# Graph layers on one core: the first six loads in halves on two queues, and one bank's identity products moved

## Chip, cores and metric

The kernel runs on one core of a Trainium2 chip. The metric is device time of one execution in microseconds (us), lower is better. The core has a matrix engine (TensorE, PE, with its weight load PEld), a vector engine (VectorE, DVE), an activation engine (ScalarE, ACT), GpSimd (POOL) and a queue engine (SyncE, SP). Loads are issued on the queues of SP and ACT, and a few on POOL's.

## The reference, cut to what matters

`x` is 16 x 1024 x 128 and `adj` is 1024 x 1024, both fp32. Layer 0 is one graph convolution with a residual and a layer norm. Layer 1 is five steps of a gated recurrent update whose messages are `adj @ h`, again with a residual and a layer norm:

```python
def _L0_gnn_ref(x, adj, weight, bias):
    support = jnp.einsum('bnf,fo->bno', x, weight)
    return jnp.einsum('nm,bmo->bno', adj, support) + bias

def step(h, _):                       # five times; in_matrix = out_matrix = adj
    m_in = jnp.einsum('nm,bmd->bnd', in_matrix, h)
    m_out = jnp.einsum('nm,bmd->bnd', out_matrix, h)
    av = jnp.concatenate([m_in, m_out], axis=-1)
    u3 = h @ u3_w.T + u3_b
    z = sigmoid(av @ w3_w.T + w3_b + u3)
    r = sigmoid(av @ w4_w.T + w4_b + u3)
    hv = tanh(av @ w5_w.T + w5_b + (r * h @ u5_w.T + u5_b))
    return (1.0 - z) * h + z * hv, None

x = _layernorm(x + _L0_gnn_ref(x, adj, L0_gnn_weight, L0_gnn_bias))
x = _layernorm(x + _L1_gnn_ref(x, adj, adj, ...))
```

## The kernel before, in words

The batch is worked in four groups of four ("quads"). For each quad the product with `adj` is done by a fast scheme in two levels with seven products each: outer matrices 1 to 7, and inside each of them inner products 1 to 7. `chain` runs the inner products of one or two outer matrices; its matrix instructions are line L410. First comes layer 0 for the four quads (chains `12_x0`, `3_x0`, `67_x0`, `54_x0` and so on), then five steps of layer 1 for each quad.

Before the first product can run, `adj` has to be on the chip and turned. It comes in eight **chunks** of 128 rows (0.524 MB each), chunks 0 to 3 into `agg`, 4 to 7 into `hid`; the rows of the first quad of `x` come as four loads of the same size, x0 to x3, into `rows`. The loop at lines 127 to 133 issues these twelve loads in the order chunk 0, chunk 1, x0, x1, chunks 2 to 7, x2, x3; the first six alternate between the queues of SP and ACT, the rest go on SP. Eight semaphores serve the loads in rotation, so that the ninth load waits in its queue for the landing of the first, the tenth for the second, and so on.

`make_identity` builds `ident` on POOL. Then PE multiplies `ident` by `ident` into three PSUM banks, `pb`, `seeded0` and `seeded1` (L212, four instructions for each bank; the trace has two records for each). This writes each bank once; later products add to these banks. After that `turn_adj(c)` (L200) turns a chunk with eight transposes into two banks `pt_adj`, four in each, and copies each bank to `a`, for chunks 0 to 3 the first on DVE (L205) and the second on ACT (L207), for chunks 4 to 7 both on ACT. Three PSUM banks take turns for this, so every fourth bank waits for the copy of the first.

PE's order in the first chain is kept as written in the program: the identity products, chunks 0 and 1, inner product 1 (called **P1** here, on `pa_x`, from chunks 0 and 1 and x0), then `first_rest` with chunks 2 and 3, inner product 2 (**P2**, on `pa_x`), then `turn_rest` with chunks 4 to 7, then inner product 5 (on `pc_x`), 6, 7, 3 and 4. P1 and P2 need chunks 0 and 1 alone; P2 stands behind the transposes of chunks 2 and 3 by its place in the order. On DVE the sums of x0 and x1 (L328 to L331) come between the copies; with L188 begins a long row of sums of the turned `adj`, of which the first waits for chunk 3. On ACT the load of a function table and a small copy `warm` (L137) follow its three load issues. L708 on ACT scales `rows` of x2 and x3 for a sum that POOL's queue completes.

Of the kernel before, what the change touches and what calls it, by code (L numbers as in the profile page):

```python
# [20 lines left out]
def kernel(  # L21
# [32 lines left out]
    nc = tc.nc  # L54
    B, N, D = x.shape
    P = 128
# [15 lines left out]
    rows = const.tile([P, QUAD, N], F32, name="rows")  # L72
# [16 lines left out]
    seeded = [ps_m.tile([P, HALF], F32, name=f"seeded{i}") for i in range(2)]  # L89
    pb = ps_m.tile([P, HALF], F32, name="pb")  # L90
# [24 lines left out]
    def x_rows(b):  # L115
        return x[b].rearrange("(p c) d -> p (c d)", c=C)
# [5 lines left out]
    queues = (nc.sync, nc.scalar)  # L122

    adj_rows = adj.rearrange("(h p n c) m -> n h p c m", h=2, n=4, c=2)
    raws = [agg[:, c] if c < CH else hid[:, c - CH] for c in range(C)]

    for i, c in enumerate([0, 1, "x0", "x1", *range(2, C), "x2", "x3"]):
        queue = queues[i % 2 if i < 6 else 0]
        if isinstance(c, str):
            k = int(c[1])  # L130
            queue.dma_start(rows[:, k], x_rows(k))
        else:
            queue.dma_start(raws[c], adj_rows[c // 2, c % 2])
    power = const.tile([P, C], F32, name="power")
    nc.vector.memset(power, -0.5)
    warm = const.tile([P, 1], F32, name="warm")
# [2 lines left out]
    ident = const.tile([P, P], F32, name="ident")  # L139
# [44 lines left out]
    def inner_left_12():  # L184
        a = [[blk[0][:, :, 2 * j : 2 * j + 2, ts(i, QT)] for j in range(2)] for i in range(2)]
        put = tc.keep_in_program_order
        (a11, a12), (a21, a22) = a
        put(nc.vector.tensor_sub(e12[:, :, 3], a11, a21))  # L188
        put(nc.vector.tensor_add(e12[:, :, 0], a21, a22))
        put(nc.vector.tensor_sub(e12[:, :, 1], e12[:, :, 0], a11))  # L190
        put(nc.vector.tensor_sub(e12[:, :, 2], a12, e12[:, :, 1]))

    def turn_adj(c):
        cols = raws[c].rearrange("p (q k) -> p k q", k=C)
        i, at = divmod(c, CH)
        for j in range(2):
            pt = bank(f"pt_adj_{c}_{j}")
            pt3 = pt.rearrange("p (k q) -> p k q", k=CH)
            for k in range(CH):
                op = nc.tensor.transpose(pt3[:, k, :], cols[:, j * CH + k, :], ident)  # L200
                if c < CH:
                    tc.keep_in_program_order(op)
            dst = blk[i][:, j, :, ts(at, P)]
            if j == 0 and i == 0:
                tc.keep_in_program_order(nc.vector.tensor_copy(dst, pt3))  # L205
            else:
                nc.scalar.copy(dst, pt3)  # L207


    for t in (pb, *seeded):  # L210
        for k in range(CH):
            nc.tensor.matmul(t[:, ts(k, P)], ident, ident, start=(k == 0), stop=True,  # L212
                             skip_group_check=True)
    for c in range(2):
        turn_adj(c)

# [525 lines left out]
        )  # L742

    def first_rest():
        for c in range(2, CH):
            turn_adj(c)
        inner_left_12()
# [184 lines left out]
    for q in range(NQ):  # L932
        for s in range(STEPS):
# [21 lines left out]
            k = s if q else s - 1  # L955
# [92 lines left out]
```

## Time and profile before

| | |
|---|---|
| median of 3 runs | 1767.29 us (1767.14 to 1767.44) |
| the profiled execution | 1767.04 us |
| its span, first to last instruction | 1765.1 us |
| granted TensorE clock | 0.999 |
| PE busy | 1755.0 us (99%) |
| DVE busy | 1302.0 us (74%) |
| ACT busy | 800.7 us (45%) |
| POOL busy | 108.2 us (6%) |
| moved by DMA | 161.86 MB, mean 92 GB/s |

The span is measured inside the execution; the 1.9 us between it and the execution's own time lie around the program. Busy time of PE is from records whose ends are modelled, so the starts of its records, and the waits of the engines around it, say more than its share. The views used below are the totals of the engines, the chain of work that ended last (the whole of it and its first 30 us), the timeline, the table by stages, and the list of load issues with the time from issue to landing.

### The profile page before, as it was taken

What the parts mean: (1) busy time and instruction counts of PE and PEld (TensorE: products, weight loads), DVE (VectorE), ACT (ScalarE), POOL (GpSimd) and SP (SyncE); (2) the same over time, 40 slices, a digit from 0 to 9 for tenths busy, and PEclk for the clock granted to TensorE, in tenths of its full rate; (3) what the DMA queues carried; (4) which work ended last, traced back from release to release, by engine and by line L of the source; (5) the groups of instructions that cost most, each with busy time, mean ns of one, the idle gap of its engine ahead of it and who ended that gap; (6) DMA issues with size and microseconds to landing.
All of it is one profiled execution on the core that took longest, in us unless ns stands there. A gap on an engine that the chain in (4) does not pass through costs nothing.

```text
span 1765.1 us, 19956 instructions
## 1 busy us (share of the span) xinstructions
PE 1755.0 (99%) x6709; PEld 1265.5 (72%) x6709; DVE 1302.0 (74%) x2286; ACT 800.7 (45%) x1425; POOL 108.2 (6%) x153
## 2 busy tenths in 40 slices
PE   9999999999999999999999999999999999999998
PEld 8888885776858577685867758586675857668584
DVE  7977777676776857777778667777778577777778
ACT  4355564344353433435354452535445353443537
POOL 2212320000000000000000000000000000000004
PEclk9999999999999999999999999999999999999999
DMA  8244354051322505143351424324243241514232
GB/s 267 72 142 144 120 142 109 12 119 33 87 67 69 140 18 136 39 119 73 83 132 60 108 60 96 87 69 119 58 110 101 55 93 26 131 25 107 60 84 95
DMA packets 405604, 161.86 MB, mean 92 GB/s; under 512 B 388352, under 2 KB 389504, under 8 KB 405504
## 3 DMA queue, kind: packets, MB, share of 16 engines
q1 hardware_dynamic: 402960, 153.01, 34.2%
q0 software_dynamic: 1968, 5.77, 1.3%
q10 hardware_dynamic: 576, 1.84, 0.3%
q8 instruction: 53, 0.87, 0.2%
q14 instruction: 47, 0.39, 0.1%
HBM read 94.51 MB, written 65.01 MB: 90 GB/s over the span
## 4 chain that ended last, share of the span: by engine, by line
PE 99%; DVE 0%; POOL 0%; POOLq 0%; issue 0%; DVEq 0%
PE pb L410 25%; PE pc L410 14%; PE pa L410 14%; PE pu L538 8%; PE ph L561 8%; PE ph L562 8%; PE pu L520 8%; PE seeded L553 8%; PE pa_x L410 3%; PE pc_x L410 3%; PE seeded L494 2%; PE pt_adj L200 0%; PE seeded L212 0%; PE pt L652 0%; PE pb L212 0%; PE pt_end L923 0%
## 5 line engine op out<-in xcount | busy, mean ns | idle before, releaser
L410 PE MATMUL pb<-e,inner 128*128 128x256 f32 x864 | 206.2, 379 | 0.0
L577 DVE TENSOR_TENSOR tsum<-tsum,hid 128x512 f32<-128x512 f32 x158 | 108.7, 688 | 106.1 <-ACT tsum L572 106.0
L572 ACT ACTIVATE tsum<-ph,bh 128x512 f32<-128x512 f32 x158 | 108.5, 687 | 164.6 <-PE ph L562 164.5
L410 PEld LDWEIGHTS pb<-e,inner 128*128 128x128 f32 x864 | 167.6, 194 | 19.0 <-ACT first L396 0.3
L538 PE MATMUL pu<-agg,w_t 128*128 128x512 f32 x320 | 163.7, 593 | 0.0
L561 PE MATMUL ph<-agg,w_t 128*128 128x512 f32 x320 | 163.4, 592 | 0.0
L553 PE MATMUL seeded<-agg,w_t 128*128 128x512 f32 x320 | 163.4, 592 | 0.0
L562 PE MATMUL ph<-tsum,u_t 128*128 128x512 f32 x320 | 163.4, 592 | 0.0
L520 PE MATMUL pu<-hid,u_t 128*128 128x512 f32 x320 | 157.0, 592 | 0.0
L541 ACT ACTIVATE tsum<-pu,br 128x512 f32<-128x512 f32 x160 | 110.0, 687 | 85.6 <-PE pu L538 85.6
L410 PE MATMUL pb<-s,inner 128*128 128x256 f32 x576 | 148.4, 380 | 0.0
L410 PE MATMUL pb<-a,inner 128*128 128x256 f32 x576 | 144.0, 379 | 0.0
L548 DVE TENSOR_TENSOR tsum<-tsum,hid 128x512 f32<-128x512 f32 x160 | 110.2, 689 | 37.7 <-ACT tsum L541 37.7
L410 PE MATMUL pc<-e,inner 128*128 128x256 f32 x560 | 133.9, 379 | 0.0
L410 PEld LDWEIGHTS pb<-s,inner 128*128 128x128 f32 x576 | 110.3, 194 | 24.8 <-issue 10.4
L556 ACT ACTIVATE tsum<-seeded,bz 128x512 f32<-128x512 f32 x160 | 110.0, 687 | 29.5 <-PE seeded L553 29.5
L410 PEld LDWEIGHTS pb<-a,inner 128*128 128x128 f32 x576 | 111.8, 194 | 12.7 <-DVE first L398 0.4
L410 PEld LDWEIGHTS pc<-e,inner 128*128 128x128 f32 x560 | 109.2, 195 | 12.8 <-issue 0.7
L562 PEld LDWEIGHTS ph<-tsum,u_t 128*128 128x128 f32 x320 | 60.8, 190 | 76.5 <-issue 58.8
L561 PEld LDWEIGHTS ph<-agg,w_t 128*128 128x128 f32 x320 | 60.6, 190 | 75.1 <-issue 74.4
L520 PEld LDWEIGHTS pu<-hid,u_t 128*128 128x128 f32 x320 | 60.8, 190 | 73.5 <-issue 72.2
L578 DVE TENSOR_TENSOR tsum<-tsum 128x512 f32<-128x512 f32 x158 | 109.2, 691 | 4.9
(197 smaller groups left out, 2860.2 us busy)
## 6 DMA issues: line engine op xcount, KB each, us to landing
turned<-ypad SPq DMA_DIRECT2D x48, 512.0 KB, 3.8
rows<-turned SPq DMA_DIRECT2D x192, 128.0 KB, 2.9
hvs<-saved SPq DMA_DIRECT2D x24, 512.0 KB, 4.0
rows<-saved SPq DMA_DIRECT2D x20, 512.0 KB, 3.7
hid<-hidden SPq DMA_DIRECT2D x64, 128.0 KB, 3.5
turned<-ypad SPq DMA_DIRECT2D x32, 256.0 KB, 2.9
rows<-turned SPq DMA_DIRECT2D x128, 64.0 KB, 2.1
hidden<-ypad SPq DMA_DIRECT2D x12, 512.0 KB, 4.1
```

The lines of the kernel that those rows point to most:

```text
L410: product = nc.tensor.matmul(bank_of[a][:, ts(o, QT)], chunk(a, o, c), left[n][a][:, c, :], start=(a in (1, 5) and o == 0 and c == 0), sto ...
L520: in_order(nc.tensor.matmul(pu, w_t["u3"], hid[:, k, ts(h, HALF)], start=True, stop=True, skip_group_check=True))
L538: in_order(nc.tensor.matmul(pu, w_t["w4"], agg[:, k, cols], start=False, stop=True, skip_group_check=True))
L541: pin(nc.scalar.activation(rh[:, cols], pu, AF.Sigmoid, bias=br))
L548: pin(nc.vector.tensor_mul(rh[:, cols], rh[:, cols], hid[:, k, cols]))
L553: in_order(nc.tensor.matmul(pz, w_t["w3"], agg[:, k, cols], start=False, stop=True, skip_group_check=True))
L556: pin(nc.scalar.activation(z_of[k % 2][:, cols], pz, AF.Sigmoid, bias=bz))
L561: in_order(nc.tensor.matmul(ph, w_t["w5"], agg[:, k, cols], start=True, stop=False))
L562: in_order(nc.tensor.matmul(ph, w_t["u5"], rh_of[k % 2][:, cols], start=False, stop=True))
L572: pin(nc.scalar.activation(hv, ph, AF.Tanh, bias=bh))
L577: pinned(nc.vector.tensor_sub(hv, hv, hid[:, k, cols]))
L578: pinned(nc.vector.tensor_mul(hv, hv, z_of[k % 2][:, cols]))
```

## The change

Each of the first six loads becomes two: the first half of the partitions (0 to 63) is issued on SP's queue, the second half (64 to 127) on ACT's. The source is divided to match; for a chunk of `adj` it is 32 of the 64 row pairs. The other six loads stay whole, on SP's queue. The identity products of `seeded1` leave their place ahead of chunk 0 and come at the start of `first_rest`, between P1 and chunk 2. They keep their place in the program's order, as do now those of the other two banks.

```diff
     for i, c in enumerate([0, 1, "x0", "x1", *range(2, C), "x2", "x3"]):
-        queue = queues[i % 2 if i < 6 else 0]
         if isinstance(c, str):
             k = int(c[1])
-            queue.dma_start(rows[:, k], x_rows(k))
+            dst, src = rows[:, k], x_rows(k)
+            halves = [src[ts(h, P // 2)] for h in range(2)]
         else:
-            queue.dma_start(raws[c], adj_rows[c // 2, c % 2])
+            dst, src = raws[c], adj_rows[c // 2, c % 2]
+            halves = [src[ts(h, P // 4)] for h in range(2)]
+        if i < 6:
+            for h, queue in enumerate(queues):
+                queue.dma_start(dst[ts(h, P // 2)], halves[h])
+        else:
+            nc.sync.dma_start(dst, src)
...
-    for t in (pb, *seeded):
+    def write_bank(t):
         for k in range(CH):
-            nc.tensor.matmul(t[:, ts(k, P)], ident, ident, start=(k == 0), stop=True,
-                             skip_group_check=True)
+            tc.keep_in_program_order(nc.tensor.matmul(
+                t[:, ts(k, P)], ident, ident, start=(k == 0), stop=True, skip_group_check=True
+            ))
+
+    write_bank(pb)
+    write_bank(seeded[0])
     for c in range(2):
         turn_adj(c)
...
     def first_rest():
+        write_bank(seeded[1])
         for c in range(2, CH):
             turn_adj(c)
         inner_left_12()
```

On the built program nothing else moves: the instructions of PE, DVE, ACT and POOL stand in the same order as before except the four of `seeded1`, and SP and ACT have three load issues more each. The loads now come as eighteen; with eight semaphores in rotation the halves of chunk 2 wait for the halves of chunk 0, those of chunk 3 for those of chunk 1, chunks 4 and 5 for the two halves of x0, chunks 6 and 7 for those of x1, and x2 and x3 for those of chunk 2.

## The prediction

> **What bounds the kernel now.** I began with the engine totals and the chain that ended last, over the whole span. This shows that TensorE (PE) carries the time; any change at the start counts only as far as it moves PE.
>
> ```profile
> PE 1755.0 (99%) x6709; PEld 1265.5 (72%) x6709; DVE 1302.0 (74%) x2286; ACT 800.7 (45%) x1425; POOL 108.2 (6%) x153
> ...
> PE 99%; DVE 0%; POOL 0%; POOLq 0%; issue 0%; DVEq 0%
> ```
>
> Then the same chain over the first 30 us (start, length, what). It is PE work from 1.35 us on, with one visible break: the VectorE (DVE) copy of chunk 1 before P1 (the first product, on `pa_x`).
>
> ```profile
> 1.35 2.08 PE pb L212 x8
> 3.43 3.41 PE seeded L212 x16
> 6.84 1.62 PE pt_adj L200 x12
> 8.47 0.02 issue
> 8.49 0.70 DVE a L205
> 9.19 0.04 issue
> 9.24 1.99 PE pa_x L410 x8
> 11.23 2.14 PE pt_adj L200 x16
> 13.37 1.73 PE pa_x L410 x8
> 15.10 3.84 PE pt_adj L200 x32
> 18.94 1.73 PE pc_x L410 x8
> ```
>
> After 26 us the timeline of PE has no gap that a load explains: product follows product at 0.216 us a record. So a shift of PE at about 15 us reaches the end undiminished. Everything that follows is: by how much does P2 (`pa_x` at 13.21 us in the timeline) move?
>
> Third, the loads. The stage table (span of time, then each engine's busy time, clock, DMA share, GB/s) says when they are limited by the transfer itself:
>
> ```profile
> 2.00:2.50 0.50, 0.50 (x4) 0.50 (x4) 0.00 (x0) 0.00 (x0) 0.00 (x0) 1.00 0.88 98
> 2.50:3.00 0.50, 0.50 (x4) 0.50 (x3) 0.00 (x0) 0.10 (x1) 0.00 (x0) 1.00 0.51 106
> 3.00:3.50 0.50, 0.50 (x5) 0.50 (x4) 0.00 (x0) 0.50 (x1) 0.00 (x0) 1.00 0.87 319
> ...
> 4.50:8.50 4.00, 4.00 (x24) 3.91 (x24) 0.70 (x2) 0.46 (x1) 0.00 (x0) 1.00 1.03 419
> 8.50:11.50 3.00, 2.83 (x15) 2.15 (x16) 2.97 (x5) 0.95 (x3) 0.00 (x0) 1.00 1.02 415
> ```
>
> Data starts at 2.0 us, is slow for 1 us (0.10 MB), then runs at 415 GB/s: 1.26 us for 0.524 MB. Issue time plus landing time of each issue gives landings at 4.8 (chunk 0), 6.1 (chunk 1), 8.5 and 9.0 (x0, x1), 11.05 and 11.5 us (chunks 2, 3). Chunk 0 lands before its turn at 6.6 us, chunk 2 at 11.05 only just in time for 11.19.
>
> **What the skill says.** The Trainium skill, *SBUF — State Buffer*, "Door 1: The DMA port swizzle": a transfer reaches ports by its partitions; 0–63 touch only 8 of 16 ports, 64–127 the other 8, at about 27.2 GB/s each, so 218 GB/s for half the partitions. All loads of before span 128 partitions, so no row shows this price. The nearest are the 32-partition fetches (`rows<-turned`): at 903.25–904.25 us, with mostly the first two of four running, the stage table has 201 GB/s, and 231 in the next microsecond when the other partitions' quarters overlap. Their 256-byte packets make this a weak sign. Same page, "Can I just issue two DMAs to hit both halves?": one transfer on each half together measured only 6% over one alone. *DMA: Bandwidth & Descriptors*, "Queues, rings and completion order": SP's and ACT's loads run on the same 16 engines, which take turns between the queues; the trace agrees, both queues' loads together make the same 415 GB/s. *TensorE: Matmul & The Clock Gate*, Part 1: PE runs at half clock until some 3.4 us of sustained work. The trace shows identity records 0.213 us apart and transposes 0.213 apart until 7.28 us, 0.111 after.
>
> **The change, part by part.**
>
> *Bank 3 moved.* Four instructions, 8 records, leave the place ahead of chunk 0 and come back after P1. At 0.213 us they gave up 1.71 us, so PE could turn chunk 0 at 4.93 instead of 6.64. But the half clock lasts to 7.28 by time: 28 records fit in before it either way (24 + 4 before, 16 + 12 after). So all eight transposes of chunk 0 and the first bank of chunk 1 run cold; what is won is 8 warm transposes, 0.9 us: the DVE copy of chunk 1 starts at 7.6 instead of 8.49, P1 at 8.34 instead of 9.24, if x0 is there. P1 takes 1.83 us to 10.17; the 8 returned records at 0.111–0.118 take 0.9, to 11.1. Chunk 2 then turns at 11.1 where it did at 11.19: **−0.1 us**, because its wait is filled. So with loads in time this part is worth nothing; its cover is the old wait for P1's copy and chunk 2. Nothing on POOL or SP moves with it; no other reader of that bank exists until the projections at 60 us.
>
> *Loads halved.* Twelve issues on SP and ACT instead of six, each 64 partitions. Issue time: SP's three took 0.65, 0.57 and 0.55 us, ACT's 0.65, 0.86 and 0.56; three more each cost about 1.8 us of queue time, on SP before chunks 4–7, which wait in the queue anyway. Eight load semaphores go round, so the halves of chunk 2 wait for chunk 0, those of chunk 3 for chunk 1, chunks 4–7 for halves of x0 and x1. On ACT the wait for chunk 1's half stands ahead of the table load (1.28 us), `warm` (0.19) and the first copies: ACT is free at 6.1 + 0.56 + 1.28 + 0.19 = 8.1 us instead of 4.4. Its copies of chunks 0 and 1 then end at 8.7 and 9.2; P1's second half asks for them at 9.31. That just fits, cost 0 to 0.3 us.
>
> The transfer is the open term. Bounds: the full 415 GB/s if the two queues stay on different ports, 218 if both queues' halves always meet on the same ports. I take 218 × 1.06 = 231 GB/s, an estimate from the page: engines take turns queue by queue, all of them started on SP's half, and a half has landed only when its slowest engine is done. Six loads are 3.146 MB. Less 0.10 MB moved by 3.0 us, 3.04 MB / 231 GB/s = 13.2 us; with 0.5 us from last packet to landing (estimate: chunk 0's share is about that), chunk 3 lands at **L = 3.0 + 13.2 + 0.5 = 16.7 us** instead of 11.5. Chunk 3's eight transposes (0.89) and a restart (0.1) put P2 at 17.7; it was at 13.2: **+4.5 us**. In this case P1 (x0 at about 9.8) and chunk 2 (about 14.4) wait too, but these waits lie ahead of L. ACT's copy of chunk 3 and DVE's L188, which start DVE's unbroken row of sums, move by the same amount. What follows at full rate still fits: chunks 4–7 land at 18.0 to 21.8 (chunk 7 is turned at 17.8 + 4.5 = 22.3); x3 at 24.4 is 0.45 late for the scaling at L708, which holds up ACT's copy L395, whose reader (the third product on `pc_x`) leaves 0.7 us: nothing.
>
> Sum: −0.1 within the wait, +4.5. Against the profiled execution: span 1765.1 → 1769.6, and 1767.04 → 1771.5 with the 1.9 us around it. The median of the runs is 1767.29, 0.25 above the profiled one: **1771.8 us**. From 0.2% on (3.5 us) a measurement of this kernel can tell from no change; that is L = 15.7, a rate of 250 GB/s.
>
> **Rivals.**
> - *A, the halves share ports* (218–250 GB/s): +5.3 to +3.5 us. For it: the page's measurements. Against: the queues differ here, and no run shows it. 0.60.
> - *B, partly overlapped* (250–345 GB/s): engines that started up to 1 us apart (the slow first microsecond) stay on opposite halves for part of the time: +3.4 to +0.2, 1767.5 to 1770.7. 0.16.
> - *C, not slower: the halves keep both sets of ports busy* (345 GB/s and up). Then L is 12.3 or less, PE never waits for chunk 3, and the sum is the bank's −0.1 with ACT's 0 to +0.3: 1767.2. For it: each queue always has a half for the other side. It decides from 345 GB/s. 0.17.
> - *D, cold clock too*: A's gaps keep PE from a sustained window before P2. Then P2's 8 records take 0.43 instead of 0.216 us (+1.7), chunk 3 +0.8, the banks of chunks 4–7 0.85 instead of ACT's 0.48 (+3): up to 1777. In A, PE still works 80% of each window up to 14 us, so 0.05.
> - *E, faster by over 3.5 us*: the chain's non-PE time between 1.35 and 19 us is below 1 us, and the cold stretch is set by time. A gain above 1 us has no source; 0.02 for what I overlook.
>
> **How the numbers follow.** Predicted 1771.8 (A). A alone is 1770.8 to 1772.6. Range 1766.9 to 1773.0: C with its 0.3 below, all of B, A; only D, E and edges are left out. Slower: 0.9 of A and D, 0.59. Faster: 0.02. Within 0.2%: C, B and A's edge, 0.39.
>
> **What would show it.** In the profile after: GB/s of 3–14 us near 230 instead of 415, and 4 KB packets longer than the 0.159 us that fills 16 engines at 415; chunk 3's transposes starting at 16–17 us; P2 at about 17.7; the distance from P2 to the end unchanged. Chunk 0 should be turned right after 16 identity records, near 5 us. The prediction is wrong if the loads keep 400 GB/s (C), if PE after chunk 3 is at 0.43 us a record (D), or if P2 moves and the end doesn't.

## The result, and the profile after

The changed kernel takes **1770.61 us** (median of 21 runs, 1769.85 to 1771.42); the kernel before, run beside it, 1767.39 us (21 runs, 1766.98 to 1768.27). The ratio is 1.0019, with a 95% interval of 1.0013 to 1.0025. So it is slower by 3.2 us, resolved from zero. It lies just within the 0.2% (3.5 us) below which the prediction would have called it no change. The profiled execution took 1770.08 us with a span of 1768.3 us: 3.04 us and 3.2 us more than before.

The engine totals and the whole chain of the kernel after:

```profile
PE 1754.3 (99%) x6709; PEld 1264.6 (72%) x6709; DVE 1302.3 (74%) x2286; ACT 800.6 (45%) x1425; POOL 113.9 (6%) x153
...
PE 98%; DMA 1%; DVE 0%; POOL 0%; issue 0%; POOLq 0%; ACT 0%; SPq 0%; DVEq 0%
```

PE does the same 6709 instructions in the same busy time. What is new is "DMA 1%" in the chain. The chain over the first 30 us says where it lies (start, length, what; L206 is L200 of before, L420 is L410, L137 is the new place of the halved load):

```profile
1.45 6.25 DMA agg<-in_adj_dram
7.70 0.02 issue
7.71 7.38 DMA agg<-in_adj_dram
15.10 0.14 issue
15.23 1.12 PE pt_adj L206 x8
16.35 1.73 PE pa_x L420 x8
18.08 3.84 PE pt_adj L206 x32
21.92 1.73 PE pc_x L420 x8
```

Before, this stretch was PE from 1.35 us on, but for one copy on DVE. Now two loads follow each other up to 15.10 us: the half of chunk 1 on SP's queue, and the half of chunk 3, which had waited in its queue for the first to land. Only then come the transposes of chunk 3 and P2. From P2 on the rows are those of before, about 3 us later.

The stage table (span of time; busy time of PE, PEld, DVE, ACT, POOL; clock, DMA share, GB/s):

```profile
2.00:2.50 0.50, 0.50 (x4) 0.50 (x4) 0.00 (x0) 0.00 (x0) 0.00 (x0) 1.00 0.44 74
2.50:3.00 0.50, 0.50 (x4) 0.50 (x3) 0.00 (x0) 0.00 (x0) 0.00 (x0) 1.00 0.68 197
3.00:3.50 0.50, 0.50 (x4) 0.50 (x4) 0.00 (x0) 0.00 (x0) 0.00 (x0) 1.00 1.06 393
4.50:8.50 4.00, 2.43 (x17) 2.00 (x17) 0.69 (x1) 1.23 (x1) 0.00 (x0) 1.00 1.00 262
8.50:11.50 3.00, 2.19 (x13) 1.85 (x12) 1.06 (x2) 1.21 (x4) 0.00 (x0) 1.00 1.08 326
11.50:14.50 3.00, 2.26 (x18) 1.88 (x16) 2.86 (x5) 0.77 (x2) 0.00 (x0) 1.00 1.03 242
14.50:18.50 4.00, 3.27 (x22) 3.09 (x23) 2.24 (x4) 1.36 (x3) 0.00 (x0) 1.00 1.00 394
```

From 3.00 us on the DMA share stays at 1.00 to 1.08, so there is always something to move. From 4.50 to 14.50 it moves at 242 to 326 GB/s, where before it moved at 415 to 419 (rows from 4.50 to 11.50). A 4 KB packet takes 214 to 276 ns there, as the mean of each of the three stages, instead of 160 to 163. Once the whole loads of chunks 4 to 7 have the engines to themselves, the rate is 394 again. PE, which was busy for 4.00 of the 4 us from 4.50 on, is busy for 2.43.

The landings, from the rows of the load issues (issue time plus time to landing, us):

| | before | after, ACT's half / SP's half |
|---|---|---|
| chunk 0 | 4.84 | 4.52 / 5.58 |
| chunk 1 | 6.10 | 6.66 / 7.70 |
| x0 | 8.50 | 9.16 / 9.64 |
| x1 | 8.96 | 10.79 / 11.01 |
| chunk 2 | 11.05 | 12.47 / 13.01 |
| chunk 3 | 11.53 | 14.32 / 15.10 |
| chunks 4 to 7 | 12.50, 13.78, 15.06, 16.33 | 16.15, 17.43, 18.71, 19.99 |
| x2, x3 | 17.61, 18.95 | 21.26, 22.61 |

### The profile page after: what moved, and what is told of

It reads as the page before. It is cut to its first block, busy times and chain, and to the rows that moved or that the text cites. A ratio compares the mean times of both kernels' runs of the same rounds, so it can differ in the third digit from the quotient of the medians.

```text
span 1768.3 us, 19966 instructions
## 1 busy us (share of the span) xinstructions
PE 1754.3 (99%) x6709; PEld 1264.6 (72%) x6709; DVE 1302.3 (74%) x2286; ACT 800.6 (45%) x1425; POOL 113.9 (6%) x153
## 4 chain that ended last, share of the span: by engine, by line
PE 98%; DMA 1%; DVE 0%; POOL 0%; issue 0%; POOLq 0%; ACT 0%; SPq 0%; DVEq 0%
PE pb L420 25%; PE pc L420 14%; PE pa L420 14%; PE pu L548 8%; PE pu L530 8%; PE seeded L563 8%; PE ph L572 8%; PE ph L571 8%; PE pc_x L420 3%; PE pa_x L420 3%; PE seeded L504 2%; DMA agg<-in_adj_dram 1%; PE pt_adj L206 0%; DVE stats L277 0%; PE pt L662 0%
## 5 line engine op out<-in xcount | busy, mean ns | idle before, releaser
L420 PE MATMUL pb<-e,inner 128*128 128x256 f32 x864 | 206.2, 379 | 0.0
L420 PEld LDWEIGHTS pb<-e,inner 128*128 128x128 f32 x864 | 167.7, 194 | 19.0 <-ACT first L406 0.3
L420 PE MATMUL pb<-s,inner 128*128 128x256 f32 x576 | 148.4, 380 | 0.0
L420 PE MATMUL pb<-a,inner 128*128 128x256 f32 x576 | 144.0, 379 | 0.0
L420 PE MATMUL pc<-e,inner 128*128 128x256 f32 x560 | 133.9, 379 | 0.0
L420 PEld LDWEIGHTS pb<-s,inner 128*128 128x128 f32 x576 | 110.4, 194 | 24.9 <-issue 10.9
L420 PEld LDWEIGHTS pb<-a,inner 128*128 128x128 f32 x576 | 111.8, 194 | 12.7 <-DVE first L408 0.4
L420 PEld LDWEIGHTS pc<-e,inner 128*128 128x128 f32 x560 | 109.2, 195 | 12.8 <-PE pu L530 0.7
L290 POOL TENSOR_SCALAR rstd<-mv 128x8 f32<-128x8 f32 (+1 forms) x32 | 10.0, 311 | 1609.0 <-DVE mv L279 1575.9
```

The lines of the kernel that those rows point to most:

```text
L420: product = nc.tensor.matmul(bank_of[a][:, ts(o, QT)], chunk(a, o, c), left[n][a][:, c, :], start=(a in (1, 5) and o == 0 and c == 0), sto ...
```

## The experiments

The question was which of the differences costs the 3.2 us: the moved bank, the number of loads, ACT's later start, or the division by partitions. All times are medians; each ratio is to the kernel before on the same chip. The loads and chains are from one profile of each kernel. Each diff shows the edit against the changed kernel, with `...` where lines are left out. "Rate" is that of the stage from 4.50 to 8.50 us, and "chunk 3" is the landing of its last part.

| kernel | us | ratio | interval | rate | chunk 3 |
|---|---|---|---|---|---|
| the change | 1770.61 | 1.0019 | 1.0013 to 1.0025 | 262 | 15.10 |
| e1, loads halved, bank not moved | 1770.84 | 1.0022 | 1.0014 to 1.0031 | 268 | 15.38 |
| e2, bank moved, loads whole | 1767.27 | 1.0001 | 0.9992 to 1.0009 | 416 | 11.66 |
| e3, halves of the columns | 1768.06 | 1.0005 | 0.9997 to 1.0013 | 374 | 12.62 |
| e5, loads whole, all on SP | 1767.04 | 0.9999 | 0.9991 to 1.0007 | 423 | 11.33 |
| e6, both halves on SP | 1772.30 | 1.0028 | 1.0017 to 1.0038 | 235 | 16.95 |
| e7, quarters, same half together | 1774.53 | 1.0041 | 1.0026 to 1.0056 | 258 | 16.06 |
| e8, quarters, opposite halves | 1773.96 | 1.0039 | 1.0024 to 1.0054 | 285 | 14.94 |
| e9, chunks 0 and 1 halved alone | 1769.82 | 1.0017 | 1.0008 to 1.0026 | 273 | 14.11 |

### e1: the loads halved, the bank where it was

```diff
     write_bank(seeded[0])
+    write_bank(seeded[1])
...
     def first_rest():
-        write_bank(seeded[1])
```

> The six loads in halves by partitions, as in the changed kernel, but all three banks of identity products ahead of chunk 0, as before. Theory (halves of the partitions share write ports, so the six loads run near 270 GB/s and chunk 3 lands near 15 us): P2 starts near 16.2 us and the time is the changed kernel's, 1770.6 us, within 0.3. Rival (the moved bank is what costs, since PE then idles ahead of chunk 0): back to 1767.4. Rival (twice as many loads): 1770.6 too.

Measured: 1770.84 us. The chain of waits has the same shape as after the change:

```profile
7.59 7.78 DMA agg<-in_adj_dram
...
15.51 1.14 PE pt_adj L206 x8
```

PE takes up chunk 3 at 15.51 us, 0.28 later than with the bank moved, and the time is 0.2 us longer, which the runs don't resolve. So the halved loads alone make the loss.

### e2: the bank moved, the loads whole

```diff
     for i, c in enumerate([0, 1, "x0", "x1", *range(2, C), "x2", "x3"]):
+        queue = queues[i % 2 if i < 6 else 0]
...
-            for h, queue in enumerate(queues):
-                queue.dma_start(dst[ts(h, P // 2)], halves[h])
...
+            queue.dma_start(raws[c], adj_rows[c // 2, c % 2])
```

> Loads whole and on two queues in turn, as before; the third bank's identity products moved behind P1. Theory (ports): loads run at 415 GB/s, P1 near 8.3 to 8.6 us (x0 lands at 8.5), the moved products fill PE's wait for chunk 2, P2 at 13.1 to 13.2, time 1767.3 us, within 0.2 of before. Rival (the moved bank costs): 1768 to 1770.

Measured: 1767.27 us, no difference from before. Stage table, and chain of waits (here L410 is L414):

```profile
4.50:8.50 4.00, 2.94 (x19) 2.28 (x18) 1.38 (x2) 1.17 (x2) 0.00 (x0) 1.00 1.02 416
```

```profile
8.91 1.97 PE pa_x L414 x8
10.88 0.89 PE seeded L212 x8
11.77 1.93 PE pt_adj L200 x16
```

The loads keep their 416 GB/s. P1 could not start at the 8.34 us of the prediction, because x0 landed only at 8.78; it gains 0.33 us on the 9.24 of before, and the 0.89 us of returned records (the moved products) then fill the wait for chunk 2 and run past it by some 0.4 us (chunk 2 landed at 11.35, and PE takes it up at 11.77). The time doesn't show this. The moved bank alone is worth nothing that can be measured.

### e3: the same twelve issues, but halves of the columns

```diff
-            halves = [src[ts(h, P // 2)] for h in range(2)]
+            halves = [src[:, ts(h, HALF)] for h in range(2)]
...
-            halves = [src[ts(h, P // 4)] for h in range(2)]
+            halves = [src[:, :, ts(h, HALF)] for h in range(2)]
...
-                queue.dma_start(dst[ts(h, P // 2)], halves[h])
+                queue.dma_start(dst[:, ts(h, HALF)], halves[h])
```

> Halves on the two queues again, twelve issues with the same waits as in the changed kernel, and the bank moved, but each half is 512 columns of all 128 partitions, with rows of 2 KB. Theory (ports): the loads run at 380 to 415 GB/s again, chunks land in order, chunk 3 near 11.5 us, P2 near 13.0, time 1767.0 to 1767.4 us. Rival (the number of loads, their semaphore waits and the late table load on ACT): 1770.6 as in the changed kernel.

Measured: 1768.06 us, a ratio of 1.0005 to before, with 1 inside the interval. Every load is cut in two, goes to the same two queues and waits for the same landings as in the change, but each half spans all 128 partitions. The stage table:

```profile
4.50:8.50 4.00, 3.49 (x23) 2.91 (x22) 1.38 (x2) 1.72 (x3) 0.00 (x0) 1.00 1.02 374
8.50:11.50 3.00, 2.34 (x14) 1.73 (x12) 1.25 (x2) 1.30 (x3) 0.00 (x0) 1.00 1.04 355
```

At 355 to 374 GB/s the last half of chunk 3 lands at 12.62 us instead of 15.10. Of the loss, 2.5 us is gone although only the direction of the cut differs, and with it the size of the packets (2 KB instead of 4 KB). This is the experiment that decides: the number of loads, the waits of the semaphores and ACT's late table load (at 6.8 us here, 7.27 after the change) are not the cause of those 2.5 us. My own theory missed by 0.7 us, though, and the chain says why:

```profile
2.98 7.04 DMA rows<-in_x_dram
...
10.22 0.70 DVE inner L338
...
14.21 1.73 PE pa_x L420 x8
```

x1's half on ACT's queue lands at 10.02 us instead of 8.96, DVE's four sums (L338 to L341) start at 10.22, its copy of a bank of chunk 3 comes behind them, and P2 starts at 14.21 instead of 13.37. The two queues had drifted apart: x0's half landed at 6.84 on SP and at 9.23 on ACT. A half that lags behind is worth nothing until its other half is there.

### e5: all loads whole and on SP

```diff
+        queue = nc.sync
...
+            queue.dma_start(rows[:, k], x_rows(k))
...
+            queue.dma_start(raws[c], adj_rows[c // 2, c % 2])
```

> All twelve loads whole and on SP's queue alone, in the old order; the third bank moved behind P1; ACT issues no load. Theory (ports): 415 GB/s, strictly in order: chunk 0 at 4.8 us, chunk 1 at 6.1, x0 at 7.4, x1 at 8.6, chunk 2 at 9.9, chunk 3 at 11.2; P2 at 13.0 to 13.2, time 1767.0 to 1767.4 us. Rival (a second queue is needed for the rate): loads below 350 GB/s and chunk 3 later than 12.5, time above 1768.

Measured: 1767.04 us, the lowest of all, but 0.25 us below before is not resolved. The stage table:

```profile
4.50:8.50 4.00, 3.66 (x20) 3.32 (x19) 1.38 (x2) 0.94 (x2) 0.00 (x0) 1.00 1.04 423
```

One queue with whole loads makes 423 GB/s, as much as two. They land in order, 1.26 to 1.29 us apart: 4.95, 6.21, 7.49, 8.78, 10.05 and 11.33. x0 is there at 7.49, a microsecond earlier than before, and P1 starts at 8.45, where the prediction had put it for loads in time (8.34). A second queue is not needed for the rate.

### e6: the same halves, both on SP's queue

```diff
-            for h, queue in enumerate(queues):
-                queue.dma_start(dst[ts(h, P // 2)], halves[h])
+            for h in range(2):
+                nc.sync.dma_start(dst[ts(h, P // 2)], halves[h])
```

> The same halves by partitions, all twelve on SP's queue, lower half then upper half of each load; bank moved. The scheduler puts P2 directly behind P1 here and a few later instructions in another order, so its time is not to be compared closely; the rate of the loads is. Theory (ports, and the second queue recovers a part by being on the other half): with one queue every engine meets the same half at about the same time, so 218 to 240 GB/s, chunk 3 after 16 us. Rival (the engines drift apart by themselves and the queue does not matter): 260 to 300 GB/s and chunk 3 near 15 us, as in the changed kernel. Rival (two queues disturb each other): 400 GB/s.

Measured: 1772.30 us. In this build P2 also stands directly behind P1; the chain then goes through chunk 3, ACT's copy and DVE's row of sums instead, so that the time says less than the loads do. The stage table:

```profile
4.50:8.50 4.00, 2.02 (x12) 1.59 (x12) 0.69 (x1) 0.59 (x1) 0.00 (x0) 1.00 0.99 235
8.50:11.50 3.00, 2.03 (x13) 1.76 (x14) 0.69 (x1) 0.59 (x1) 0.00 (x0) 1.00 1.03 249
```

The low and the high half one after the other make 235 to 251 GB/s from 4.50 us on, and chunk 3 lands at 16.95. By the formula of the prediction this is 3.04 MB / (16.95 - 3.5) = 226 GB/s; the change, by the same formula, has 3.04 / (15.10 - 3.5) = 262. By this measure the second queue with the opposite half wins 16%, much less than the doubling that both halves always moving side by side would have brought.

### e7 and e8: quarters that meet on the same half, or on opposite halves

Both cut each of the six loads into four of 32 partitions, two on each queue, and differ in the order alone: in e7 the two queues send neighbouring quarters of one half at the same time, in e8 quarters of opposite halves.

```diff
...
-            halves = [src[ts(h, P // 4)] for h in range(2)]
+            parts = [src[ts(j, P // 8)] for j in range(4)]
...
-            for h, queue in enumerate(queues):
-                queue.dma_start(dst[ts(h, P // 2)], halves[h])
+            for n, j in enumerate((0, 1, 2, 3)):        # e8: (0, 2, 1, 3)
+                queues[n % 2].dma_start(dst[ts(j, P // 4)], parts[j])
```

> The six loads in quarters of 32 partitions: SP takes 0-31 and then 64-95, ACT takes 32-63 and then 96-127, so the two queues are always on the same half of the partitions. Bank moved. ACT has twelve issues ahead of its table load, so its copies are late; the rate of the loads is what is compared. Theory (ports): both queues share 8 ports all the time, 200 to 225 GB/s, chunk 3 near 17 us. Rival (transfers of fewer partitions are slow each by itself, whatever runs beside them): the same rate as in the kernel of quarters on opposite halves.

> The same quarters of 32 partitions, but SP takes 0-31 and 32-63, ACT 64-95 and 96-127: the queues are on opposite halves, as in the changed kernel. Theory (ports): the engines' turns between the queues keep both sets of ports in use for part of the time, 250 to 300 GB/s, chunk 3 at 14.5 to 16 us, clearly earlier than with the queues on the same half. Rival (each transfer by itself is slow): no difference between the two kernels.

Measured: 1774.53 and 1773.96 us, not told apart by the runs (1774.24 to 1775.05 and 1773.76 to 1775.38). The loads differ more: e8 starts at 285 GB/s where e7 has 258, and its chunk 3 lands at 14.94 instead of 16.06. In sign this is what opposite halves should do, and e8's 285 and 14.94 lie in the ranges expected of it. e7 missed its own: it has 247 to 258 GB/s from 4.50 us on and not 200 to 225. A difference of 10% in one stage doesn't exclude the rival, that transfers of few partitions are slow each by itself. Nor does the time tell, for with 24 issues the loads no longer set the end. The stage table and the chain of e7:

```profile
8.50:11.50 3.00, 2.78 (x11) 2.09 (x9) 0.69 (x1) 0.00 (x0) 0.00 (x0) 0.50 1.02 247
11.50:14.50 3.00, 0.65 (x3) 0.08 (x1) 2.54 (x4) 2.45 (x4) 0.00 (x0) 0.50 1.01 250
```

```profile
11.91 1.28 ACT L143
13.21 0.19 ACT warm L143
13.40 0.98 ACT a L213 x2
14.42 2.07 PE pa_x L420 x4
```

ACT issues twelve loads, and the table load (L143) stands behind the last of them, which waits for a landing; so it starts at 11.91 us (2.90 before), ACT's copies of chunks 0 and 1 end at 14.4, and P1's second half waits for them. PE, which had idled before chunk 1, is at half its clock from 7.7 to 17.9 us, as the clock records and the distance of its own records show. So P1's second half takes 2.07 us for 4 records. Here the ACT step that the prediction put at 0 to 0.3 us is seen at work, and the slow clock of rival D, though it falls on P1 and the moved bank and not on P2. In e8 the table load starts at 11.74, and its DMA share falls below 1 besides:

```profile
8.50:11.50 3.00, 2.45 (x10) 1.63 (x9) 0.73 (x2) 0.00 (x0) 0.00 (x0) 1.00 0.81 242
```

At a share of 0.81 the engines are not always busy; its 242 GB/s is no measure of what opposite halves can do.

### e9: only chunks 0 and 1 halved

```diff
-        if i < 6:
+        if i < 2:
             for h, queue in enumerate(queues):
...
-            nc.sync.dma_start(dst, src)
+            queues[i % 2 if i < 6 else 0].dma_start(dst, src)
```

> Only chunks 0 and 1 in halves by partitions on the two queues; x0, x1, chunks 2 and 3 whole and on the queues in turn; bank moved. Theory (ports): 1.05 MB at 270 instead of 415 GB/s loses 1.4 us, then full rate; chunk 3 lands near 12.9 instead of 11.5 and P2 starts near 13.9 instead of 13.2: time 1768.0, +0.4 to +1.0 us. Rival (a fixed cost of dividing, whichever loads it is): 1770 and more.

Measured: 1769.82 us, a loss of 2.5 where 0.4 to 1.0 was expected. This is the expectation that missed most. The stage table and the chain:

```profile
4.50:8.50 4.00, 3.11 (x14) 2.42 (x14) 0.69 (x1) 1.12 (x3) 0.00 (x0) 1.00 1.03 273
8.50:11.50 3.00, 3.00 (x12) 2.47 (x11) 0.69 (x1) 0.59 (x1) 0.00 (x0) 1.00 1.02 407
```

```profile
8.00 1.97 PE pt_adj L206 x8
9.97 2.38 PE pa_x L420 x8
...
15.57 1.73 PE pa_x L420 x8
```

Chunk 1 lands at 7.95 instead of 6.10 (+1.85). I had expected the whole loads behind it to keep most of their dates; but they stand in the same queues and move by as much, and ACT's queue falls behind: chunk 3, on ACT, lands at 14.11 (+2.6), just ahead of SP's chunk 4 at 14.30 (+1.8), which was issued after it. At 407 GB/s from 8.50 us on, there was no spare rate to make up what the first two loads had lost. The time is close to that of the rival, a fixed cost of dividing (1770 and more). Against the rival stand the 407 GB/s once the whole loads run, and e3, where twelve divided loads cost 0.8 us that isn't resolved. PE also stayed at half pace to about 10.9 us in this profile: chunk 1's eight transposes take 1.97 us, and P1 takes 2.38 instead of 1.99.

## Why the prediction was right or wrong, point by point

- **PE bounds, a shift of P2 reaches the end undiminished:** right. P2 started 2.98 us later (16.19 instead of 13.21), the first product on `pc_x` 2.98 later (21.75 instead of 18.775), the products after 200 us 3.05 later, the span is 3.2 longer.
- **The bank is worth -0.1 us:** right in size; e2 measured no difference, and e1 against the change 0.2 us that isn't resolved. The working under it took the date of the half clock's end from before ("28 records fit in before it either way", to 7.28 us). e5 nearly kept that date (7.5), but after the change chunk 0's transposes, from 5.71 us on, are already 0.111 us apart, and in e2 full pace begins at 5.5. That the bank was still worth nothing then rests on the waits for x0 and chunk 3, not on this step.
- **ACT's late start costs 0 to 0.3 us:** right at nothing in the change. ACT's table load started at 7.27 and its first copy at 8.66, 0.56 later than the step had it, because the step took chunk 1's landing of before (6.1) where the slowed half landed at 6.66; but P1 waited for x0 (9.64) and started at 9.78. With four parts instead of two this cover is gone, as e7 shows.
- **The loads slow down, and P2 follows L by 1.0 us:** right. P2 followed the landing of chunk 3 by 1.09 us.
- **The rate, 218 × 1.06 = 231 GB/s, L = 16.7 us:** this term was mis-sized. It was 262 GB/s by the same formula, L = 15.10 us, 1.6 us earlier, and so +2.98 instead of +4.5. By this formula the halves in turn on one queue (e6) have 226 GB/s, close to the 218, and the second queue added 16% and not 6%: it is the second factor that was mis-sized. The formula itself is rough. Over 3 to 15 us the engines moved 279 GB/s or 3.35 MB, more than the six loads hold, so part of chunk 4 was already among it. And it was not SP's half that the engines began with: all 33 packets up to 3.00 us are of ACT's queue. x0 came nearly as predicted (9.64, predicted 9.8), chunk 2 1.4 us before its predicted 14.4, and chunks 4 to 7 1.8 us before theirs.
- **The rivals:** by rate and time this is rival B (250 to 345 GB/s, 1767.5 to 1770.7), at its slow end, given 0.16; A's own range began at 1770.8. The measured time lies in the stated range because the range took in B and C, not because A, the case it was centred on (0.60), came true. The two are one mechanism, told apart by how often the halves meet, and I had taken the page's 6% whole although the prediction itself says that the queues differ here. C (the halves keep both sides busy) fell: it needed 345 GB/s over the whole stretch. Only the stage from 8.5 to 11.5 came near, with 326. D did not happen after the change, although PE worked only 2.43 of the 4 us from 4.50 on (61%, where D counted on 80%); its slow clock was seen in e7.

**What is shown, and what isn't.** Shown: the division by partitions costs the time (e1 has it alone, e2 lacks it), and the number of divided loads doesn't, but for the 0.8 us that e3 leaves unresolved. That the cause is the ports of the Trainium skill's *SBUF — State Buffer*, "Door 1: The DMA port swizzle", fits: 235 to 251 GB/s for halves in turn, more when opposite halves run together (the change against e6, e8's start against e7), 415 to 423 for whole loads over all 128 partitions. But it is argued and not shown. No record shows a port. e3 differs in one more thing, its packets of 2 KB instead of 4 KB, and no run changes the partitions without changing which part of the source is read together.

Open also is why the change had 326 GB/s in one stage and 242 in the next. If queues that drift in and out of opposite halves explain it, the rate should go with the shares of the engines' time that the two queues have. The traces say so only in part (a queue's share is the time of its packets over that of 16 engines; packets overlap a little, so two shares can add up to more than 100%):

| stretch, us | queues on | SP's share | ACT's share | GB/s |
|---|---|---|---|---|
| the change, 5.0 to 6.5 | opposite halves | 68.5% | 30.0% | 227 |
| the change, 8.0 to 9.5 | opposite halves | 57.2% | 51.7% | 382 |
| e1, 8.0 to 9.5 | opposite halves | 53.8% | 48.5% | 300 |
| e7, 8.0 to 9.5 | the same half | 51.9% | 51.1% | 254 |
| the change, 3.0 to 3.4 | opposite halves | 28.0% | 74.7% | 389 |

The first four rows fit: even shares are fast on opposite halves and not on the same half. The last doesn't: the engines spent three quarters of their time on ACT's half and still moved 389 GB/s, for 0.4 us. And with even shares the change and e1 are far apart. So the shares alone don't set the rate, and the cause of its swings stays open.

## What to carry to other kernels

Where a load has to be divided, divide it so that each part still covers all 128 partitions (by columns it kept 355 to 374 GB/s here, by partitions 242 to 326), and look at the rate in GB/s beside the DMA share: a full share at 63% of the rate (262 of 419 here) tells that the engines are busy but slow. At the start of this PE-bound kernel the landing of the last chunk that the first products wait for set the loss; so order the loads as they are needed before dividing any. One queue with whole loads was as fast here as two, and with two queues the parts drifted apart. Moving PE work into a wait that a load will end anyway was worth nothing that could be measured.

## What the runs showed of the hardware that was not expected

- The end of PE's half pace at the start is no fixed time: the first records at full pace came at 7.40 us before, by 5.7 after the change, at 4.6 in e1, 5.5 in e2, 5.2 in e3, 7.5 in e5, 6.2 in e6, 4.4 in e7 and only at 10.6 in e8 and 10.9 in e9, one profile each. During that start the clock column reads 1.00 although the records stand 0.213 us apart; when e7's PE was slowed later it reads 0.50.
- Two queues that are given equal parts in turn do not advance evenly: x0's column halves landed 2.39 us apart in e3 (6.84 and 9.23), the two halves of chunk 0 in the change 1.06 apart (4.52 and 5.58).
